# Two-layer transformer: layer 1's second and third block go to the experts as one group, experts at half the rate beside the last two attentions

## Chip, cores and metric

The kernel runs on one core of a Trainium2 chip. The metric is the device time of one execution in microseconds (us); less is better. Engines: PE (matrix multiply, with its weight loads as PEld), DVE (vector), ACT (scalar), POOL (gather and scatter issue, a few small operations), SP (issues the direct transfers).

## What is computed

The input is 8 sequences of 256 tokens with 128 features, 2048 tokens in all. Two layers follow, each an attention and a mixture of experts with 8 experts, of which every token takes two. Cut to what matters here (layer 1; layer 0 has a softmax attention and Gelu experts):

```python
x = x + _L1_attn_ref(_layernorm(x), ...)        # linear attention, 16 heads, segments of 32
x = x + _L1_ffn_ref(_layernorm(x), ...)

def _L1_ffn_ref(x, gate_w, gate_b, w1, b1, w2, b2):
    probs = softmax(xt @ gate_w + gate_b)
    _, idx = top_k(probs, 2)
    mask = one_hot(idx, 8).sum(axis=1) > 0
    h1 = relu(einsum('th,ehf->etf', xt, w1) + b1)     # 128 -> 512 for each expert
    out_e = einsum('etf,efh->eth', h1, w2) + b2       # 512 -> 128
    return einsum('eth,te->th', out_e, mask)
```

## The kernel before

**Blocks and slots.** The 2048 tokens are four blocks of 512 (`NBLK`, four tiles of 128 rows each, `NT`). Layer 1's attention of a block needs that block's layer 0 to be done, and nothing of other blocks. For the experts, the tokens of a block are sorted by expert into slot tiles of 128 rows: `dispatch` (line 380) counts with small matmuls how many tokens chose each expert, gives every expert whole tiles, and works out each token's two rows. 512 tokens with two choices fill at most 2·4 + 8 − 1 = 15 tiles (`SL`), since each expert's last tile may be part empty; the kernel always computes all 15. Eight indirect transfers on POOL (line 433) scatter the rows into a buffer in memory, `xg[h]`; the buffers were filled with zeros at the start.

**A slot tile.** `experts` (line 469) is a generator. Its first step starts the load of four tiles of rows (`xr`, line 477) and the weights of two tiles; its second turns the rows (four transposes on PE, line 487, and a copy on DVE, line 488). Then comes one step for each tile and one more at the end: load the weights of the tile two ahead (`weigh`, two transfers of 256 KB, whose address is read from `half.expert`), four matmuls into the hidden layer (line 508; in f32 each is recorded as two, so 8 a tile), four activations on ACT (line 515), and the second matmuls of the tile before (line 520). After every fourth tile the results are copied out of the accumulator on DVE (line 528) and written to `yg[h]` (line 531). 15 tiles take 18 steps. The row load waits for all scatters of its block.

**Back from the experts.** `chosen` (line 563) gathers each token's two result rows by 8 indirect transfers on POOL (line 569). In layer 0 `combine0` adds them and `before1` prepares layer 1's attention (projections, scores with the segment means, about eight steps); in layer 1 `finish` adds them (line 1349) and stores the block.

**The order of the work.** Each engine runs its instructions in the order in which the program issues them, nearly so at least, and the program chooses that order with two queues (`Lines`, line 1274): "chain" holds routing, gathers, combining and preparing, "experts" the expert generators, one after another. The attentions are generators too: `attention1` (line 1058) has 9 parts (sums, scores of tile 0 to 3 with values and heads one part behind, then `retrieved` for tiles 0 to 3). After each part, `beside` calls `go`:

```python
def go(self, time, chain, experts):
    for _ in range(chain):
        self.now += time / chain
        ...
        self.step("chain")
        self.credit = min(self.credit + experts / chain, 2.0)
        while self.credit >= 1.0:
            self.step("experts")
            self.credit -= 1.0
```

`PART1 = (1.5, 3, 2.0)` stands for layer 1: three chain steps and two expert steps after each part, so 18 expert steps beside one attention, just one block's. A step whose due time has not come is passed over. After the attention of block b, `routed(b, 1)` joins the chain (statistics, logits, the two best experts, `dispatch`), and three time units after its experts are known, its generator may run. The last attention over, `go(*PART1)` runs until both queues are empty; this is called the tail below.

Layer 0's experts run beside layer 0's attention and the first two attentions of layer 1. Layer 1's blocks 0 and 1 go beside attentions 2 and 3, blocks 2 and 3 come in the tail.

Of the kernel before, what the change touches and what calls it, by code (L numbers as in the profile page):

```python
# [54 lines left out]
SL = 2 * NT + E - 1  # L56
# [11 lines left out]
    "before": P, "ones": P, "cap": E * NT, "upto": E * E, "slot": SL, "index": E,  # L68
# [11 lines left out]
def two_layers(  # L80
# [163 lines left out]
    def slots_of_zeros():  # L244

        nc.gpsimd.memset(zero, 0.0)
        for h in range(NBLK):
            xg.append(tl(dram, [SL * P, D], f"xg{h}"))
            rows = xg[h].rearrange("(t p) d -> p t d", p=P)
            filled.append([])  # L250
            for t in range(0, SL, SG):
                n = min(SG, SL - t)
                filled[h].append(
                    nc.sync.dma_start(
                        out=rows[:, t : t + n, :],
                        in_=zero.unsqueeze(1).to_broadcast([P, n, D]),
                    ).ins
                )
            yg.append(tl(dram, [SL * P, D], f"yg{h}"))

# [108 lines left out]

    class Block:  # L370


        def __init__(self, b):
            self.h = b
            self.experts_known = False
            self.rows = tl(wk, [P, NT, D], "hrows")
            self.hots = tl(wk, [P, 2, NT, E], "hhots")
            self.gates = tl(wk, [P, 2, NT], "hgates", bufs=NBLK)

    def dispatch(half, b1s):  # L380

        h1, h2 = half.hots[:, 0], half.hots[:, 1]
        m, tot = small("chosen", (P, NT, E)), small("total", (P, E))
        nc.vector.tensor_tensor(m, h1, h2, ALU.add)
        nc.vector.tensor_reduce(tot, m.rearrange("p t e -> p e t"), AX.X, ALU.add)
        yield
        pr = bank()
        rank = pr[:, 0 : NT * E].rearrange("p (t e) -> p t e", e=E)
        with behind(PE):
            nc.tensor.matmul(rank, lhsT=const("before"), rhs=m, start=True, stop=False)  # L390
            for t in range(NT - 1):
                n = NT - 1 - t
                nc.tensor.matmul(
                    rank[:, t + 1 :, :], lhsT=const("ones"),
                    rhs=m[:, t, :].unsqueeze(1).to_broadcast([P, n, E]),
                    start=False, stop=(t == NT - 2),
                )
            pc = bank()
            nc.tensor.matmul(pc[:, 0:E], lhsT=const("ones"), rhs=tot, start=True, stop=True)

        c3, tiles = small("cap3", (P, E, NT)), small("tiles", (P, E))
        nc.vector.tensor_tensor(
            c3, last(pc[:, 0:E], NT), const("cap").rearrange("p (e c) -> p e c", e=E), ALU.is_gt
        )
        nc.vector.tensor_reduce(tiles, c3, AX.X, ALU.add)
        u3, ends, starts = small("upto3", (P, E, E)), small("ends", (P, E)), small("starts", (P, E))
        nc.vector.tensor_tensor(
            u3, tiles.unsqueeze(1).to_broadcast([P, E, E]),
            const("upto").rearrange("p (e c) -> p e c", e=E), ALU.mult,
        )  # L410
        nc.vector.tensor_reduce(ends, u3, AX.X, ALU.add)
        nc.vector.tensor_tensor(starts, ends, tiles, ALU.subtract)

        base, pos = small("base", (P, E)), small("pos", (P, NT, E))
        nc.vector.tensor_scalar_mul(base, starts, float(P))
        nc.vector.tensor_tensor(
            pos, rank, base.unsqueeze(1).to_broadcast([P, NT, E]), ALU.add
        )
        ph, at = small("posk", (P, 2, NT, E)), small("at", (P, 2, NT))
        nc.vector.tensor_tensor(  # L420
            ph, half.hots, pos.unsqueeze(1).to_broadcast([P, 2, NT, E]), ALU.mult
        )
        nc.vector.tensor_reduce(at, ph, AX.X, ALU.add)
        half.slots = tl(wk, [P, 2, NT], "slots", mybir.dt.uint32, NBLK)
        nc.vector.tensor_copy(half.slots, at)  # L425
        yield

        xg_h = xg[half.h]
        half.sent = []
        key = f"sent{next(names)}"  # L430
        for t in range(NT):
            for k in range(2):
                i = nc.gpsimd.indirect_dma_start(  # L433
                    out=xg_h[:, :],
                    out_offset=bass.IndirectOffsetOnAxis(ap=half.slots[:, k, t : t + 1], axis=0),
                    in_=half.rows[:, t, :], in_offset=None,
                ).ins
                tc.declare_no_dep(i, group=key, reason="slots of their own")
                tc.add_to_no_dep_group(key, i)
                for f in filled[half.h]:  # L440
                    tc.add_manual_dep(i, f.name, SYNC, reason="after zeros")
                half.sent.append(i)
            if t % 2:
                yield

        sl = const("slot").unsqueeze(2).to_broadcast([P, SL, E])
        o1, o2 = tl(wk, [P, SL, E], "own1", bufs=1), tl(wk, [P, SL, E], "own2", bufs=1)
        nc.vector.tensor_tensor(o1, starts.unsqueeze(1).to_broadcast([P, SL, E]), sl, ALU.is_le)
        nc.vector.tensor_tensor(o2, ends.unsqueeze(1).to_broadcast([P, SL, E]), sl, ALU.is_gt)
        nc.vector.tensor_tensor(o1, o1, o2, ALU.mult)  # L450
        nc.vector.tensor_tensor(
            o2, o1, const("index").unsqueeze(1).to_broadcast([P, SL, E]), ALU.mult
        )
        of = small("of", (P, SL))
        nc.vector.tensor_reduce(of, o2, AX.X, ALU.add)
        half.expert = tl(wk, [P, SL], "expert", mybir.dt.int32, NBLK)
        nc.vector.tensor_copy(half.expert, of)
        half.bias = tl(wk, [P, SL, NC], "bias", bufs=NBLK)
        b4 = tl(wk, [P, SL, NC, E], "bias4", bufs=1)
        nc.vector.tensor_tensor(  # L460
            b4, o1.unsqueeze(2).to_broadcast([P, SL, NC, E]),
            b1s.rearrange("p (e c) -> p c e", c=NC).unsqueeze(1).to_broadcast([P, SL, NC, E]),
            ALU.mult,
        )
        nc.vector.tensor_reduce(half.bias, b4, AX.X, ALU.add)
        half.experts_known = True
        yield

    def experts(half, w1, w2, func):

        x_rows = xg[half.h].rearrange("(t p) d -> p t d", p=P)
        y_rows = yg[half.h].rearrange("(t p) d -> p t d", p=P)

        def load(t0):
            n = min(SG, SL - t0)
            xr = tl(wk, [P, SG, D], "xr")
            i = nc.sync.dma_start(out=xr[:, 0:n, :], in_=x_rows[:, t0 : t0 + n, :]).ins
            for s in half.sent:
                tc.add_manual_dep(i, s.name, SYNC, reason="rows sent")
            return xr  # L480

        def turned(xr, t0):
            n = min(SG, SL - t0)
# [7 lines left out]
        def weigh(s):  # L491
            e = nc.values_load(
                half.expert[0:1, s : s + 1], engines=(mybir.EngineType.SP,),
# [9 lines left out]
        def hidden(s, xrT):  # L503
# [9 lines left out]
            for c in range(NC):  # L513
                src, bias = ph[:, c * P : (c + 1) * P], half.bias[:, s, c : c + 1]
                nc.scalar.activation(hT[:, c, :], src, func, bias=bias)  # L515
# [9 lines left out]
        def store(po, t0):  # L525
            n = min(SG, SL - t0)
# [13 lines left out]
        for s in range(SL + 1):  # L540
            if s + AHEAD < SL:
                weigh(s + AHEAD)
            if s < SL:
# [3 lines left out]
                if t0 < SL:  # L547
# [5 lines left out]
            if prev is not None:  # L553
# [4 lines left out]
                if t == SG - 1 or s == SL:  # L558
                    store(po, s - 1 - t)
# [3 lines left out]
    def chosen(half):  # L563

        half.yt = yt = tl(wk, [P, 2, NT, D], "yt")
        for t in range(NT):
            with behind(POOL):
                for k in range(2):
                    nc.gpsimd.indirect_dma_start(  # L569
                        out=yt[:, k, t, :], out_offset=None, in_=yg[half.h][:, :],  # L570
                        in_offset=bass.IndirectOffsetOnAxis(
                            ap=half.slots[:, k, t : t + 1], axis=0
# [306 lines left out]
    def route0(x, half):  # L879
# [17 lines left out]
        half.acc = acc = tl(wk, [P, NT, D], "acc", bufs=NBLK)  # L897
# [4 lines left out]
        yield from dispatch(half, b1s0)  # L902
# [347 lines left out]
    def route1(x, half):  # L1250
# [13 lines left out]
        yield from dispatch(half, b1s1)  # L1264
# [53 lines left out]
    PART0, PART1 = (2.0, 4, 1.5), (1.5, 3, 2.0)  # L1318

    SENT, STORED, BACK = 3, 2, 2  # L1320
    lines, linear = Lines(), {}

    def to_experts(b, half, layer):
        w1, w2, func = ((w1_0, w2_0, AF.Gelu), (w1_1, w2_1, AF.Relu))[layer]
        lines.add("experts", experts(half, w1, w2, func), SENT, lambda: gather(b, half, layer))
# [29 lines left out]
    def routed(b, layer):  # L1355
# [3 lines left out]
        half = Block(b)  # L1359
        sent = (route0, route1)[layer](xs[b], half)  # L1360
        for _ in sent:
            yield
            if half.experts_known:
                to_experts(b, half, layer)
                half.experts_known = False
# [13 lines left out]
    def layer1(b):  # L1379
        while b not in linear:  # L1380
            lines.go(*PART1)
        beside(attention1(linear[b], xs[b]), PART1)
# [10 lines left out]
def shape_constants():  # L1393
# [35 lines left out]
    c["cap"] = np.broadcast_to(P * np.arange(NT), (P, E, NT))  # L1429
# [52 lines left out]
```

## Time and profile before

| | us |
|---|---|
| median of 4 runs | 702.98 (700.52, 700.56, 705.40, 706.04) |
| the profiled execution | 699.48 |
| its span, first to last instruction | 697.7 |

| engine | busy us | share of the span |
|---|---|---|
| PE | 568.4 | 81% |
| PEld (weight loads, beside PE) | 424.6 | 61% |
| DVE | 406.7 | 58% |
| ACT | 333.9 | 48% |
| POOL | 189.9 | 27% |

The mean granted PE clock is 0.923 of full speed. The transfers moved 95.8 MB, 240 x 256 KB of it expert weights. Where things stand in the span: the first scores of layer 1's four attentions (line 1125) start at 322.0, 387.7, 461.5 and 541.4 us; layer 1's scatters start at 439.3, 497.2, 560.3 and 620.7 us, its gathers at 539.3, 601.9, 646.5 and 683.1 us. The last expert matmul ends at 678.5 us.

How to read the lines: a group of instructions has its line, engine, operation, tiles written and read, partitions x elements, count, then busy us and mean ns of one, then the engine's idle time ahead of them and what ended it. Busy times of matmuls overlap in part, since they are pipelined; the busy time of a stretch counts every moment once. The chain of waits follows the work back from the instruction that ended last, at each step to what released it. "issue" is time in which the engine waited for nothing that the profile shows.

### The profile page before, as it was taken

To read this page: it belongs to the slowest core of one execution; us is meant where nothing else is said; L and a number is where in the kernel's file an instruction comes from. 1 tells how busy PE (TensorE), PEld (TensorE's weight loads), DVE (VectorE), ACT (ScalarE), POOL (GpSimd) and SP (SyncE) were. 2 spreads that over 40 slices of the span, in tenths; PEclk is the share of its full clock that TensorE was granted. 3 is DMA by queue.
4 is the path that set the end of the run, shared out by engine and by line. 5 is a ranking of instruction groups with operands and counts; after the bars stand their busy time and mean duration, and the time that the engine had idled before them with its cause. 6 is when DMAs were issued, how large, how long until landed. Compare 5 with 4: busy or idle time off the path is not lost.

```text
span 697.7 us, 13688 instructions
## 1 busy us (share of the span) xinstructions
PE 568.4 (81%) x4846; PEld 424.6 (61%) x4846; DVE 406.7 (58%) x1193; ACT 333.9 (48%) x761; POOL 189.9 (27%) x223
## 2 busy tenths in 40 slices
PE   4777786998989788976899769979988899887880
PEld 3233343667546456645688547757867789886770
DVE  3665666526746556526687378787887776651110
ACT  2142443686958579852555214643345324433340
POOL 4210115002154111441204430415422440431404
PEclk9899989898999899997999979998999979999995
DMA  6700003453254414452435714455565547778861
GB/s 165 209 20 1 1 1 104 143 177 104 62 177 140 129 46 122 122 166 74 132 92 159 223 59 132 147 166 162 156 178 152 176 151 216 234 228 252 263 200 54
DMA packets 132099, 95.81 MB, mean 137 GB/s; under 512 B 8816, under 2 KB 114368, under 8 KB 132032
## 3 DMA queue, kind: packets, MB, share of 16 engines
q1 hardware_dynamic: 127520, 85.58, 41.5%
q0 software_dynamic: 4096, 8.40, 4.1%
q10 hardware_dynamic: 416, 0.96, 0.5%
q8 instruction: 39, 0.64, 0.4%
q14 instruction: 28, 0.23, 0.1%
HBM read 77.87 MB, written 17.04 MB: 136 GB/s over the span
## 4 chain that ended last, share of the span: by engine, by line
PE 46%; DVE 18%; POOL 9%; issue 9%; ACT 9%; DMA 7%; SPq 1%; POOLq 0%; ACTq 0%; DVEq 0%
PE mm L508 10%; PE mm L520 8%; PE sc L790 7%; POOL xg L433 4%; POOL yt L569 3%; DVE at L1130 2%; PE sc L981 2%; DMA yt<-yg,slots 2%; ACT hT L515 2%; ACT at L737 2%; PE sc L1125 2%; DMA w<-in_w 2%; PE mm L1143 2%; POOL rsqrt L277 1%; PE mm L1162 1%
## 5 line engine op out<-in xcount | busy, mean ns | idle before, releaser
L515 ACT ACTIVATE hT<-mm,bias 128x128 f32<-128x128 f32 x480 | 136.3, 371 | 130.3 <-PE mm L508 121.7
L508 PE MATMUL mm<-xrT,w 128*128 128x128 f32 x960 | 137.4, 290 | 18.5 <-DVE xrT L488 12.1
L508 PEld LDWEIGHTS mm<-xrT,w 128*128 128x128 f32 x960 | 123.4, 201 | 33.6 <-DVE xrT L488 16.8
L520 PE MATMUL mm<-w,hT 128*128 128x128 f32 x960 | 136.2, 283 | 5.9 <-ACT hT L515 5.8
L520 PEld LDWEIGHTS mm<-w,hT 128*128 128x128 f32 x960 | 122.4, 196 | 16.1 <-ACT hT L515 14.4
L433 POOL DMA_INDIRECT xg<-hrows,slots x64 | 66.0, 1032 | 109.6 <-DVE slots L425 57.2
L569 POOL DMA_INDIRECT yt<-yg,slots x64 | 61.2, 956 | 102.7 <-DMA yg<-ys 46.1
L737 ACT ACTIVATE at<-sc 128x1024 f32<-128x1024 f32 x48 | 48.8, 1023 | 56.5 <-PE sc L790 56.3
L790 PE MATMUL sc<-qm,kxT 32*128 32x512 f32 x192 | 52.9, 660 | 11.0 <-ACT at L737 4.5
L790 PE MATMUL sc<-km,qT 32*128 32x512 f32 x192 | 54.7, 703 | 3.3 <-DVE qx L698 1.7
L277 POOL TENSOR_TENSOR rsqrt<-rsqrt,mhalf 128x4 f32<-128x4 f32 (+1 forms) x20 | 18.5, 926 | 124.8 <-DVE rsqrt L276 71.3
L698 DVE TENSOR_REDUCE nmax<-sc 128x8 f32<-128x1024 f32 x32 | 38.9, 1221 | 22.7 <-PE sc L790 22.7
L1130 DVE TENSOR_TENSOR at<-sc,consts 128x1024 f32<-128x1024 f32 x32 | 38.1, 1216 | 8.5 <-PE sc L1125 8.2
L515 ACT ACT_TABLE_LOAD x25 | 32.1, 1283 | 13.6 <-PE mm L508 13.2
L528 DVE COPY ys<-mm 128x512 f32<-128x512 f32 (+1 forms) x32 | 20.9, 654 | 30.2 <-PE mm L520 25.0
L790 PEld LDWEIGHTS <-identb 32*32 32x32 bf16 (+1 forms) x320 | 7.8, 92 | 41.0 <-issue 39.5
L1068 POOL TENSOR_TENSOR vm<-va,consts 128x432 f32<-128x432 f32 x16 | 14.6, 932 | 58.2 <-ACT hT L515 19.7
L748 PE MATMUL mm<-at,vx 128*32 128x512 f32 x192 | 26.4, 624 | 4.6 <-ACT at L737 4.6
L790 PEld LDWEIGHTS sc<-qm,kxT 32*128 32x128 f32 x192 | 14.2, 188 | 24.6 <-issue 9.3
L488 DVE COPY xrT<-mm 128x512 f32<-128x512 f32 (+1 forms) x32 | 20.9, 653 | 14.1 <-PE mm L487 14.0
L1149 ACT COPY rope<-mm 128x512 f32<-128x512 f32 x16 | 9.4, 588 | 40.5 <-PE mm L1143 40.5
L1125 PE MATMUL sc<-pqm,kT 32*128 32x512 f32 x128 | 22.1, 764 | 7.3 <-DVE at L1130 4.9
(212 smaller groups left out, 945.1 us busy)
## 6 DMA issues: line engine op xcount, KB each, us to landing
w<-in_w SPq DMA_DIRECT2D x240, 256.0 KB, 3.0
xr<-xg SPq DMA_DIRECT2D x24, 256.0 KB, 4.0
yg<-ys SPq DMA_DIRECT2D x24, 256.0 KB, 2.3
xg<-zero SPq DMA_DIRECT2D x12, 256.0 KB
xr<-xg SPq DMA_DIRECT2D x8, 192.0 KB, 2.4
yg<-ys SPq DMA_DIRECT2D x8, 192.0 KB, 5.0
x<-in_x SPq DMA_DIRECT2D x4, 256.0 KB, 5.5
xg<-hrows,slots POOLq DMA_INDIRECT x64, 2.2
```

What stands on the lines that cost most here:

```text
L277: nc.gpsimd.tensor_tensor(r, r, mhalf[:, 0:n], ALU.pow)
L433: i = nc.gpsimd.indirect_dma_start(out=xg_h[:, :], out_offset=bass.IndirectOffsetOnAxis(ap=half.slots[:, k, t : t + 1], axis=0), in_=half. ...
L508: nc.tensor.matmul(ph[:, c * P : (c + 1) * P], lhsT=w1s[:, c * P : (c + 1) * P], rhs=xrT[:, t * P : (t + 1) * P], start=True, stop=True,)
L515: nc.scalar.activation(hT[:, c, :], src, func, bias=bias)
L520: nc.tensor.matmul(po[:, t * D : (t + 1) * D], lhsT=hT[:, c, :], rhs=w2s[:, c, :], start=(c == 0), stop=(c == NC - 1),)
L569: nc.gpsimd.indirect_dma_start(out=yt[:, k, t, :], out_offset=None, in_=yg[half.h][:, :], in_offset=bass.IndirectOffsetOnAxis(ap=half.slot ...
L698: return nc.vector.tensor_reduce(nm[:, js[0] : js[0] + 2, :], sc.rearrange("p j (i k) -> p j i k", i=G), AX.X, ALU.max, negate=True,)
L737: return nc.scalar.activation(pT[:, js[0] : js[0] + 2, :], sc, AF.Exp)
L748: nc.tensor.matmul(self.po[32 * j : 32 * j + 32, :], lhsT=self.vx[:, kt, j, :], rhs=self.pT_of[s][:, j, :], start=(kt == 0), stop=(kt == qt),)
L790: done[n].append(nc.tensor.matmul(*args, **kw))
L1125: nc.tensor.matmul(sc[j].rearrange("p (i k) -> p i k", i=G), lhsT=pkT[rows, cols], rhs=pqm[rows, :, cols], start=True, stop=True,)
L1130: nc.vector.tensor_tensor(at[:, 2 * a : 2 * a + 2].rearrange("p j i k -> p (j i) k"), d.rearrange("p j (i k) -> p (j i) k", i=G), const("t ...
```

## The change

Layer 1's blocks 1 and 2 are dispatched together. `GROUPS` lists the groups of blocks of each layer; layer 0 keeps one block for each. A `Group` holds the two one-hot choices of all its tiles, and its blocks write their part. `dispatch` runs once for a group, after its last block is routed: with 8 tiles of tokens it has 8 ranking matmuls in place of 4 and one more for the totals, and 16 scatters. 1024 tokens with two choices fill at most 2·8 + 8 − 1 = 23 slot tiles, against 15 + 15. Block 3 is on its own as before. When the group's experts are done, the gathers of both blocks join the chain.

The experts' rate beside the attentions of blocks 2 and 3 falls from two steps a part to one (`PART2`); in the tail it stays two. The buffer `xg1` grows to 23 tiles, so does `yg1`, with two more zero transfers; the constants grow by 40 columns; `acc`, layer 0's accumulator, has three buffers in place of four.

```diff
+GROUPS = (((0,), (1,), (2,), (3,)), ((0,), (1, 2), (3,)))
+MT = NT * max(len(g) for gs in GROUPS for g in gs)
+def slot_tiles(nt):
+    return 2 * nt + E - 1
-SL = 2 * NT + E - 1
+SL = slot_tiles(MT)
...
+    class Group:
+        def __init__(self, h, blocks):
+            self.h, self.blocks, self.parts = h, blocks, []
+            self.nt = NT * len(blocks)
+            self.sl = slot_tiles(self.nt)
+            self.experts_known = False
+            self.hots = tl(wk, [P, 2, MT, E], "hhots")[:, :, 0 : self.nt]
...
-    def dispatch(half, b1s):
+    def dispatch(group, b1s):
+        nt, sl = group.nt, group.sl
...
-            for t in range(NT - 1):
-                n = NT - 1 - t
+            for t in range(nt - 1):
+                n = nt - 1 - t
...
-        for t in range(NT):
+        for t in range(nt):
             for k in range(2):
                 i = nc.gpsimd.indirect_dma_start(
...
-                    in_=half.rows[:, t, :], in_offset=None,
+                    in_=group.parts[t // NT].rows[:, t % NT, :], in_offset=None,
...
-        for s in range(SL + 1):
-            if s + AHEAD < SL:
+        for s in range(sl + 1):
+            if s + AHEAD < sl:
                 weigh(s + AHEAD)
...
-        half.acc = acc = tl(wk, [P, NT, D], "acc", bufs=NBLK)
+        half.acc = acc = tl(wk, [P, NT, D], "acc", bufs=3)
...
-        yield from dispatch(half, b1s1)
+        if half.last:
+            yield from dispatch(half.group, b1s1)
...
-    PART0, PART1 = (2.0, 4, 1.5), (1.5, 3, 2.0)
+    PART0, PART1, PART2 = (2.0, 4, 1.5), (1.5, 3, 2.0), (1.5, 3, 1.0)
...
+        def then():
+            for b, half in zip(group.blocks, group.parts):
+                gather(b, half, layer)
+        lines.add("experts", experts(group, w1, w2, func), SENT, then)
...
-        beside(attention1(linear[b], xs[b]), PART1)
+        beside(attention1(linear[b], xs[b]), PART1 if b < 2 else PART2)
```

## The prediction

> **What bounds the kernel now.** I read the busy time by stretch first, then the chain of waits inside the stretches that the change touches, then their costliest groups, then TensorE's timeline where the stretches meet. Everything up to the end of the second layer-1 attention is issued in the same order by both kernels, so the question starts at 463 us. From 463 to 596 us the last two layer-1 attentions run (blocks 2 and 3), with expert tiles between their steps; from 596 to 680 us there are only expert tiles and the routing of block 3; then come the last gather and store. Columns: stretch, length, busy time of PE, PEld, DVE, ACT and POOL, then granted clock, DMA share, GB/s.
>
> ```profile
> 450.00:500.00 50.00, 42.83 (x443) 35.28 (x442) 42.01 (x122) 20.19 (x55) 14.84 (x16) 0.93 0.51 152
> 463.00:500.00 37.00, 31.19 (x348) 25.97 (x346) 29.65 (x94) 10.99 (x35) 14.84 (x16) 0.91 0.43 127
> 536.00:596.00 60.00, 57.33 (x589) 49.98 (x588) 41.29 (x110) 22.46 (x72) 17.89 (x18) 0.91 0.62 182
> 463.00:596.00 133.00, 119.36 (x1201) 101.84 (x1199) 99.32 (x284) 49.77 (x154) 44.87 (x44) 0.94 0.56 165
> 596.00:640.00 44.00, 36.06 (x295) 34.85 (x295) 19.87 (x64) 17.80 (x62) 17.07 (x17) 0.96 0.78 234
> 640.00:680.00 40.00, 32.00 (x249) 30.07 (x247) 6.18 (x11) 17.11 (x60) 7.61 (x8) 0.96 0.79 239
> ```
>
> In the attentions PE is busy 119.4 of 133 us and DVE 99.3 (0.747 of it; the first row is the most that DVE reaches in any 50 us, 0.84). So PE is the fuller engine, with DVE close behind. In the tail DVE has little to do. Line 508 has 8 matmuls per slot tile; of that line alone the same stretches hold
>
> ```profile
> 463.00:596.00 133.00, 34.17 (x240) 30.83 (x240) 0.94 0.56 165
> 596.00:680.00 84.00, 34.67 (x240) 31.23 (x240) 0.96 0.78 236
> ```
>
> so 30 tiles lie beside the two attentions and 30 in the tail. The chain of waits tells the two attentions apart. The first answer is for 463 to 541 us (attention of block 2), the second for 541 to 597 us (block 3):
>
> ```profile
> by line: PE mm L508 11.6%; issue 7.5%; DVE at L1130 7.3%; PE mm L520 6.6%; POOL xg L433 5.2%; PE sc L981 4.4%; POOL rsqrt L277 4.0%; DVE cand L348 3.2%; DVE vm L1206 3.2%; PE sc L1125 2.7%; DVE hrows L296 2.5%; DVE acc L924 2.2%; DVE hr L12
> ```
>
> ```profile
> by line: PE mm L508 22.9%; PE mm L520 22.9%; issue 10.2%; PE sc L1125 9.3%; PE mm L1143 8.3%; PE mm L1162 8.0%; PE sc L1198 3.4%; PE mm L487 3.2%; ACT hT L515 3.0%; PE mm L587 1.9%; PE mm L602 1.8%; PE mm L1157 1.6%; PE mm L362 1.4%; PE mm
> ```
>
> In the first, expert matmuls are 18% of the chain and DVE's steps carry it; in the second they are 46%. Last, the groups of 463 to 596 us that price a tile:
>
> ```profile
> L520 PE MATMUL mm<-w,hT 128*128 128x128 f32 x247 | 34.9, 281 | 1.9 <-ACT hT L515 1.9
> L508 PE MATMUL mm<-xrT,w 128*128 128x128 f32 x240 | 34.2, 289 | 3.5 <-DVE on L1171 1.5 <-issue 1.3 <-DVE xrT L488 0.8
> L487 PE MATMUL mm<-ident,xr 128*128 128x128 f32 x34 | 5.9, 298 | 0.0
> L528 DVE COPY ys<-mm 128x512 f32<-128x512 f32 (+1 forms) x8 | 5.2, 652 | 1.0 <-PE mm L520 1.0
> L488 DVE COPY xrT<-mm 128x512 f32<-128x512 f32 (+1 forms) x8 | 5.2, 652 | 0.2 <-PE mm L487 0.2
> ```
>
> A tile there costs PE (34.9 + 34.2 + 5.9)/30 = 2.5 us and DVE 10.4/30 = 0.35 us.
>
> **Where the tiles go.** I walked the two queues by the rules in `go` and `step`. Before, the experts of layer-1 blocks 0 and 1 (15 + 15 tiles) fall beside attentions 2 and 3, as the trace has it. After, blocks 1 and 2 are sent only when block 2 is routed, which happens beside attention 3; until then only block 0's 15 tiles exist, and at one step per part nine of them fall beside attention 2 and six beside attention 3. The other 23 + 15 = 38 tiles come in the tail. So the attentions lose 15 tiles and the tail gains 8: the 7 saved tiles are worth something only if the attentions shrink by more than the tail grows.
>
> **The tail: dearer.** Block 3's tiles alone run from 639.4 us (first line-508 matmul) to 678.5 us: 39.1/15 = 2.61 us a tile, PE, weight transfers and row loads together. Eight more: +20.9 us. Bounds: 2.0 us where nothing waits (seven tiles from 598.8 to 612.7 us), +16; 84/30 = 2.8 with routing among them, +22.4. I take 2.61 because most of the new tiles run with no routing beside them. The gather of block 0 (8 indirect DMAs, about 1.25 us each on POOL) and its additions (line 1349, 1.6 us of DVE) also move there, under tiles that last 60 us: nothing, or at most +2 from shared DMA engines; without that cover, 11 us.
>
> **Attention 2: cheaper.** Taking 6 of 15 tiles out of the chain of 463 to 541 us (lines 508 and 520: 9.0 + 5.1 us in it) gives 5.6. The dispatch of block 1 goes from here: its four scatters in the chain with the gaps between them (4.1 + 0.9), which POOL ran ahead of a `rsqrt` that layer 0's last combine waited for, and 2.4 us of its small DVE steps. Together 13.
>
> **Attention 3: cheaper, but DVE is next.** Nine of 15 tiles out of the second chain (12.8 + 12.8 + 1.8 + 1.7 us of lines 508, 520, 487 and 515) would give 17.5. But from 536 to 596 us DVE is busy 41.3 us; nine tiles take 3.1 from it, block 0's additions 1.6, and the wider dispatch (23/15 on lines 448 to 465) adds 1.9: 38.5. At the 0.80 that DVE reaches from 463 to 500 us this needs 48 us of the 60: 12 given back. I take 11.
>
> Both checked together by DVE over 133 us: 99.3 - 15 x 0.35 - 5.6 (one dispatch: half of the paired rows of lines 384 to 465) + 1.9 - 1.6 = 88.8 us of work. At 0.747 that lasts 118.9 us (14 back), at 0.80 it lasts 111 (22 back), at 0.84 105.7 (27 back). PE's own rest, 119.4 - 37.5 + 0.9 (four more dispatch matmuls) = 83 us, is below. My 24 back is a DVE share of 0.815, between the 0.80 of the stretch itself and its best 50 us.
>
> The Trainium skill speaks against this move (Perfetto Trace Analysis, Optimization Strategy): where the fullest engine changes from stretch to stretch, interleaving those stretches can help. The rows above show just that, DVE at 0.75 beside the attentions and near 0.15 from 640 us on, and the change un-mixes eight tiles; by the rule alone the sign would be slower.
>
> **Where they meet.** Before, the tail's first tile waits for its turned rows: PE stood 2.7 us until 598.8 us, under few steps. After, the order is the last `retrieved`, block 3's statistics, then the first turn, with no other tile in flight: the DVE steps ahead (line 1206 twice, lines 1212 and 1215, four statistics) are some 4.5 us. +2.5, between 0 and +5. SP's first row load and both weight loads behind it wait for 16 scatters, at 1.27 us start to start 20 us and 2.2 to land; they start where block 2's did, 19 us after the first scores (541.4 to 560.3), or a little sooner, and so land about 41 us after them, while attention 3 should last 46: hidden by some 5 us.
>
> **The granted clock** was 0.50 from 557 to 567 us, after a PE wait of only 1.9 us (553.2 to 555.0), and that cost some 5 us of PE work. Fewer tiles mean more such waits, on a stretch where DVE would bind: I take 0, up to +5. The skill (TensorE: Matmul & The Clock Gate, The HAM clock gate) has the clock halved after an idle window of about 3.4 us; here a shorter gap came before it, and by the rule fewer windows would be lost than I allow.
>
> Nothing else costs: two more zero transfers of 256 KB for the longer `xg1` and 40 more constant columns land before 100 us, where the DMA share from 50 to 100 us is 0.00. `acc` with 3 buffers makes block 3 wait for block 0's combine, over since about 230 us when block 3 is routed at 348.
>
> **Sum** against the profiled execution (699.48 us, span 697.7): -13 - 11 + 20.9 + 2.5 + 0.5 = 0. The median of the runs is 3.5 above it, 702.98; I forecast 703. By the bounds, the attentions give back 14 to 37 and the tail with its start costs 16 to 30.
>
> **The rivals.** *Faster:* PE alone sets the attentions. For it: PE is busy 90%, and the chain of attention 3 is nearly all PE. Against: DVE would have to work 88.8 us in 95.5, 0.93, which it does nowhere. 37.5 back against 23.4: -14, 689 us. It decides from 30 us given back. *Slower:* the attentions run at the pace of their own DVE steps, each waiting for the one before through PE, ACT or POOL, so that DVE's share stays at 0.747 and only 14 us come back, while 23.4 are added: +9.5, 712 us; at 0.76, above it. Place: 463 to 596 us. For it: DVE's 33 us are the largest part of attention 2's chain, with 8.5 of POOL and 5.7 of issue. Against: a third of PE's work leaves the same stretch. *Late rows:* the 16 scatters end after attention 3 and the tail starts dry; 6 us more than my sum if routing comes late by 11: 709 us. It also caps the first rival. That the tiles are not fewer can be ruled out: 15 + 23 + 15 is written out in `slot_tiles`.
>
> **How the numbers follow.** Forecast 0.41 (697 to 708), faster 0.25, slower 0.25, late rows 0.09 (some half of it over 1%). One per cent, 7 us, is about what a measurement of this kernel can tell from no change. So faster 0.25, within 0.46, slower 0.29. Leaving out a tenth on either side, the range runs from 691 us, inside the faster case, to 714 us, inside the slower one.
>
> **What would show it.** Line 508 has 904 matmuls, some 304 of them in the tail. From the first line-1125 matmul of attention 2 (461.5 us) to the tail's first line-508 matmul there are 137 us now; 115 would be right, under 105 the first rival, over 122 the second. DVE's share there should rise to about 0.8 and the chain of attention 3 should turn from PE to DVE. From the first tile of the tail to the end there are 99 us now; 120 would be right, and a tail at 2.0 us a tile would make me wrong by 5. A first row load that waits for scatters well past attention 3 would show the third.

## The result and the profile after

The changed kernel takes 705.15 us (median of 52 runs), the kernel before 702.92 (78 runs): a ratio of 1.0021 with a 95% interval of 1.0004 to 1.0038. Run again beside other kernels it stood at 1.0079 (1.0048 to 1.0110). So there is no gain, and a loss of some 0.2 to 0.8%. The two intervals do not overlap, so a ratio can shift between sessions by more than its interval says, here by 0.6%. The lines below are from a profiled execution with a span of 706.9 us; line numbers are those of the changed kernel, 24 or 25 higher around the experts (508 is 533, 520 is 545, 487 is 512, 569 is 594).

The stretches, cut where the last two attentions begin (first scores of attention 2) and where the tail's first expert tile starts. Columns: stretch, length, busy time of PE, PEld, DVE, ACT and POOL, granted clock, DMA share, GB/s; then the same for line 533 alone (PE and PEld only).

```profile
468.20:579.80 111.60, 92.77 (x953) 73.72 (x953) 92.26 (x263) 34.06 (x96) 36.05 (x36) 0.91 0.35 103
579.80:706.90 127.10, 86.24 (x676) 83.37 (x676) 28.89 (x79) 43.90 (x154) 39.14 (x41) 0.85 0.70 212
```

```profile
468.20:579.80 111.60, 17.39 (x120) 15.52 (x120) 0.91 0.35 103
579.80:706.90 127.10, 44.80 (x304) 40.85 (x304) 0.85 0.70 212
```

Cut in the same way, the kernel before has 137.3 us (461.5 to 598.8) and 98.9 us (to 697.7). The attentions hold 15 tiles instead of 30 and are 25.7 us shorter; the tail holds 38 instead of 30 and is 28.2 us longer. (In the first profiled execution of the changed kernel, with a span of 709.9 us, the attentions take 116.9 us and the tail 128.0; attention 2 alone took 73.1 us there at a granted clock of 0.81, and 66.9 here at 0.90.) DVE's share beside the attentions is 92.26/111.6 = 0.83. The chain of waits of the two attentions, 468 to 535 us and 535 to 580 us:

```profile
by line: issue 11.8%; PE mm L533 8.2%; DVE at L1156 7.0%; PE sc L1151 6.2%; PE mm L545 5.2%; PE sc L1007 5.1%; DVE vm L1232 5.1%; DVE hr L1238 3.2%; DVE hhots L363 2.5%; POOL norms L986 2.5%; PE mm L1169 2.2%; DVE probs L1031 1.7%; DVE xl L
```

```profile
by line: DMA yg<-ys 10.3%; DVE vm L1232 9.3%; PE mm L533 8.7%; PE mm L1169 6.0%; DVE hr L1238 5.7%; DVE at L1156 5.3%; PE mm L545 5.0%; PE sc L1151 4.9%; issue 4.5%; PE mm L1188 4.4%; PE mm L417 3.4%; ACT hT L540 2.5%; DVE cand L361 2.3%; P
```

In the second, expert matmuls fell from 46% to 14% and DVE's steps lead, but the first entry is new: a store of expert results, `yg<-ys`. It leads to where the tail's extra time is. TensorE's timeline where the tail begins (start, duration, operation, count; in brackets the idle time before it and what ended that):

```profile
577.12 1.09 PE L512 MATMUL mm<-ident,xr 128*128 128x128 f32 x4 [1.56 <-DMA xr<-xg]
579.81 3.78 PE L533 MATMUL mm<-xrT,w 128*128 128x128 f32 x16 [1.60 <-DVE xrT L513]
583.39 1.32 PE L545 MATMUL mm<-w,hT 128*128 128x128 f32 x8
595.47 1.16 PE L324 MATMUL mm<-ident,hrows 128*128 128x128 f32 x4 [10.76 <-DVE hrows L308]
```

After two tiles TensorE stands for 10.76 us: its next instruction in order is the transpose of block 3's normalized rows (line 324, line 312 before), and the other 36 tiles stand behind it. (In the first profiled execution the same wait is 11.12 us.) `hrows` needs POOL's `rsqrt`. POOL's timeline (line 457 is a scatter, 594 a gather, 289 the `rsqrt`), then the issues of SP's queue:

```profile
551.63 2.09 POOL L457 DMA_INDIRECT xg<-hrows,slots  x1 [8.04 <-DVE slots L449]
...
571.70 0.96 POOL L457 DMA_INDIRECT xg<-hrows,slots  x1 [0.30 <-issue]
584.12 0.98 POOL L594 DMA_INDIRECT yt<-yg,slots  x1 [11.47 <-DMA yg<-ys]
...
592.92 0.94 POOL L594 DMA_INDIRECT yt<-yg,slots  x1 [0.30 <-issue]
593.88 1.06 POOL L289 TENSOR_TENSOR rsqrt<-rsqrt,mhalf 128x4 f32<-128x4 f32 x1
```

```profile
558.49 0.34 SPq L522 DMA_DIRECT2D w<-in_w  x1
574.09 0.92 SPq L502 DMA_DIRECT2D xr<-xg  x2
...
578.70 0.46 SPq L556 DMA_DIRECT2D yg<-ys  x1
```

Read from SP on: the group's first row load (line 502) waits for the sixteen scatters, and SP issues nothing from 558.5 to 574.1 us. Block 0's last result store (line 556) stands behind it and goes out at 578.70. The store's data were ready at 572.2 us, when their copy on DVE (line 553) ended; the row load and five weight transfers then went ahead of it, and from its issue to the first gather 5.4 us passed, with a DMA share of 0.96 from 578 to 584 us. Block 0's gathers, next on POOL, wait 11.47 us for that store. Block 3's `rsqrt`, whose operands were ready at 579.2 us, stands behind the eight gathers and runs at 593.88; the last of its operands on VectorE was

```profile
579.00 0.17 DVE L288 TENSOR_SCALAR rsqrt<-mv 128x4 f32<-128x4 f32 x1
```

In the kernel before, that `rsqrt` ran ahead of the gather:

```profile
599.44 1.04 POOL L277 TENSOR_TENSOR rsqrt<-rsqrt,mhalf 128x4 f32<-128x4 f32 x1 [28.57 <-DMA w<-in_w]
601.94 1.02 POOL L569 DMA_INDIRECT yt<-yg,slots  x1 [1.46 <-ACT hT L515]
```

The kernel before has a like knot elsewhere, where layer 1 begins. There the PE, the SP and the POOL timelines read:

```profile
407.90 1.12 PE L312 MATMUL mm<-ident,hrows 128*128 128x128 f32 x4 [9.51 <-DVE xrT L488]
```

```profile
378.00 1.74 SPq L477 DMA_DIRECT2D xr<-xg  x2
380.47 0.44 SPq L531 DMA_DIRECT2D yg<-ys  x1
385.59 0.46 SPq L531 DMA_DIRECT2D yg<-ys  x1
```

```profile
375.63 0.95 POOL L433 DMA_INDIRECT xg<-hrows,slots  x1 [0.30 <-issue]
391.30 0.98 POOL L569 DMA_INDIRECT yt<-yg,slots  x1 [14.71 <-DMA xr<-xg]
...
402.79 1.04 POOL L277 TENSOR_TENSOR rsqrt<-rsqrt,mhalf 128x4 f32<-128x4 f32 x1
```

Scatters, a row load ahead of stores, gathers, `rsqrt`, and a PE wait of 9.51 us on `hrows`. (The label names VectorE's last earlier step; the `rsqrt` at 402.79 shows what was late. The gather's wait is labelled with the row load; that it too waited for the store of 385.59 is read from the order.)

### The profile page after: what moved, and what is told of

Same layout as the page of the kernel before. It is cut to its first block, busy times and chain, and to the rows that moved or that the text cites. A ratio compares the mean times of both kernels' runs of the same rounds, so it can differ in the third digit from the quotient of the medians.

```text
span 709.9 us, 13319 instructions
## 1 busy us (share of the span) xinstructions
PE 567.1 (80%) x4725; PEld 419.4 (59%) x4725; DVE 400.1 (56%) x1169; ACT 326.6 (46%) x733; POOL 188.5 (27%) x223
## 5 line engine op out<-in xcount | busy, mean ns | idle before, releaser
L540 ACT ACTIVATE hT<-mm,bias 128x128 f32<-128x128 f32 x452 | 129.1, 373 | 130.2 <-PE mm L533 125.8
L533 PE MATMUL mm<-xrT,w 128*128 128x128 f32 x904 | 132.1, 293 | 18.5 <-DVE xrT L513 14.0
L533 PEld LDWEIGHTS mm<-xrT,w 128*128 128x128 f32 x904 | 118.7, 205 | 31.3 <-DVE xrT L513 16.6
L545 PE MATMUL mm<-w,hT 128*128 128x128 f32 x904 | 130.3, 287 | 2.3 <-ACT hT L540 2.0
L545 PEld LDWEIGHTS mm<-w,hT 128*128 128x128 f32 x904 | 117.8, 200 | 11.6 <-ACT hT L540 9.9
L815 PE MATMUL sc<-qm,kxT 32*128 32x512 f32 x192 | 55.0, 683 | 11.1 <-ACT at L762 4.6
L815 PE MATMUL sc<-km,qT 32*128 32x512 f32 x192 | 56.8, 726 | 3.2 <-DVE qx L723 1.7
L513 DVE COPY xrT<-mm 128x512 f32<-128x512 f32 (+1 forms) x30 | 19.6, 655 | 18.2 <-PE mm L512 18.1
L308 DVE TENSOR_SCALAR hrows<-x,mv,rsqrt 128x128 f32<-128x128 f32 x32 | 9.2, 344 | 36.4 <-POOL rsqrt L289 36.4
```

Source lines behind the costliest of these rows:

```text
L533: nc.tensor.matmul(ph[:, c * P : (c + 1) * P], lhsT=w1s[:, c * P : (c + 1) * P], rhs=xrT[:, t * P : (t + 1) * P], start=True, stop=True,)
L545: nc.tensor.matmul(po[:, t * D : (t + 1) * D], lhsT=hT[:, c, :], rhs=w2s[:, c, :], start=(c == 0), stop=(c == NC - 1),)
L815: done[n].append(nc.tensor.matmul(*args, **kw))
```

## The experiments

Theory A: the stall at the start of the tail is a queue of orders, and taking it away gives its time back. Rival B: the tail is bound tile by tile, and a wait taken away returns elsewhere. All ratios are to the kernel before in the same session, with 95% intervals. The profiled executions of the group at the full rate and of the later gather are about 1% longer than the medians of their kernels, that of both orders at the full rate 0.6%; their lines are read for order and waits more than for length. Where a stretch is given, "attentions" runs from the first scores of attention 2 to the tail's first tile, "tail" from there to the end of the span.

**The changed kernel again**, unedited, as the measure for the others.

> The changed kernel as it is, for a second profile. Theory A (a new wait eats the gain): PE stands for 10 us or more once at the start of the tail, between the first two tiles of the group and the turning of block 3's rows, because block 0's eight gathers are ahead of block 3's rsqrt on POOL; about 115 us from the first scores of attention 2 to the first tile of the tail, and 0 to +3 us on the kernel before in the median. Rival B (the predicted balance: attentions give back some 20 us, the tail costs about as much tile by tile): that wait belongs to one execution, here it is under 4 us, and the tail is long because a tile costs 2.6 us and more all along.

708.37 us, 1.0079 (1.0048 to 1.0110); the profile shown above. The wait is there again, as theory A has it; the time is 5.5 us above the kernel before instead of 0 to 3.

**Both orders at once.** The gather of block 0 two time units later, so that the `rsqrt` stands ahead of it on POOL; and every group's first row load placed in SP's order where the code issues it, behind the last store of the group ahead (`behind(SP)` keeps it from being moved forward).

```
-        lines.add("chain", chosen(half), STORED, use)
+        lines.add("chain", chosen(half), STORED + 2 * (layer == 1 and b == 0), use)
...
-            i = nc.sync.dma_start(out=xr[:, 0:n, :], in_=x_rows[:, t0 : t0 + n, :]).ins
+            with behind(SP) if t0 == 0 else nullcontext():
+                i = nc.sync.dma_start(out=xr[:, 0:n, :], in_=x_rows[:, t0 : t0 + n, :]).ins
```

> Two orders altered and no work taken away: block 0's gather is due two time units later, so that block 3's rsqrt is ahead of it on POOL; and the group's first row load stands behind block 0's last store on SP. Theory A: the 11 us wait at the start of the tail is gone, and the time falls by 9 to 13 us against the changed kernel, to 0.98 to 0.985 of the kernel before (690 to 694 us). Rival B: the wait moves on to the next row load or weight load, the time stays within 4 us of the changed kernel.

680.9 us, 0.9694 (0.9641 to 0.9747): the sign of theory A with over twice its size. The stall is gone, but attention 2's first scores also came at 448.0 us instead of 468.2, ahead of the place. The next runs take the edit apart.

**The group at the full rate, and half the rate without the group.** The change has two parts; each alone:

```
-        beside(attention1(linear[b], xs[b]), PART1 if b < 2 else PART2)
+        beside(attention1(linear[b], xs[b]), PART1)
```

> The group of 23 tiles without the half rate: two expert steps beside the last two attentions too. Block 0's 15 tiles then all lie beside attention 2, none beside attention 3, and block 0's gather comes beside attention 3, far ahead of the tail. Theory A: no 11 us wait at the start of the tail, so it is 4 to 10 us faster than the changed kernel, although attention 3 has no tiles to fill it. Rival B: an attention 3 without tiles stands on its own DVE steps and saves too little, so it is slower than the changed kernel by 3 to 10 us.

```
-GROUPS = (((0,), (1,), (2,), (3,)), ((0,), (1, 2), (3,)))
+GROUPS = (((0,), (1,), (2,), (3,)), ((0,), (1,), (2,), (3,)))
```

> The half rate without the group: four blocks of 15 tiles, one expert step a part beside the last two attentions. 15 tiles lie beside them and 45 in the tail. Both theories: the tail grows by 15 tiles of 2.6 us (39 us), the attentions give back 15 to 20 us, as DVE paces them and block 1's dispatch stays where it was; 18 to 26 us slower than the kernel before, 1.025 to 1.037. If tiles in the tail cost 2.0 us, only 8 to 12 us slower.

The group at the full rate: 694.05 us, 0.9857 (0.9801 to 0.9913). It too holds 15 tiles beside the attentions (116.8 us) and 38 after them, but block 0's tiles end sooner: their last store goes out at 537.9 us, ahead of the scatters, there is no 11 us wait (TensorE waits 5.79 us for the group's rows instead), and the tail takes 114.8 us. Half the rate without the group: 720.07 us, 1.0243 (1.0174 to 1.0313), with 15 tiles beside (125.3 us) and 45 in a tail of 132.6; the attentions give back 12.0 us and the tail grows by 33.7, where 15 to 20 and 39 were expected. So the grouping gains; the half rate alone only moves fifteen tiles to the tail, and beside the group it is what puts block 0's last store behind the row load.

**The two orders one by one**, in the changed kernel. First only the later gather:

> The changed kernel with one order different: block 0's eight gathers are taken up two time units later, so that block 3's rsqrt stands ahead of them on POOL. Theory A (the 11 us in which PE waits at the start of the tail for block 3's rows are the queue POOL gather -> rsqrt): that wait is gone or under 2 us, the row load of the group still holds SP for some 15 us, and the time is 9 to 12 us below the changed kernel, 693 to 697. Rival B (the tail is bound by the balance of its tiles, a wait taken away comes back tile by tile): 702 to 706, as the changed kernel. Between: the waiting row load holds the last result store and the first weights, a third of the gain is given back, 698 to 701.

699.72 us, 0.9973 (0.9935 to 1.0011). The transpose of line 324 goes without a wait, but SP is still held until 579.87, and a new wait of 4.32 us for the dispatch of block 3 stands at 605.00:

```profile
589.77 0.66 PE L324 MATMUL mm<-ident,hrows 128*128 128x128 f32 x4
...
605.00 2.07 PE L533 MATMUL mm<-xrT,w 128*128 128x128 f32 x8 [4.32 <-DVE cap L426]
```

Of the 9 to 12 us that A expected it shows 3.4 by the ratio to 1.0021 and 7.4 by that to 1.0079; the case named in between came true.

Then only the row load, and only the group's (`t0 == 0 and group.nt > NT` as the condition in the edit above). On PE, POOL and VectorE the order of instructions is exactly that of the changed kernel, and on SP only this load stands elsewhere:

> The changed kernel with one transfer at another place on SP: the first row load of the group of two blocks stands behind block 0's last result store; PE, POOL and VectorE keep their order. Theory A: the store goes out 10 to 15 us earlier, the gathers run under the group's scatters' landing, the rsqrt is early, the 11 us wait is gone, time 693 to 697. Rival B: 702 to 706. If the 27 us that both edits together brought come from this place alone, it would be 678 to 684; I expect not, since in that kernel the first scores of attention 2 began 14 to 20 us earlier than in the changed kernel, ahead of this place.

693.92 us, 0.9901 (0.9870 to 0.9931), inside what A expected and outside what B did. SP's, POOL's and TensorE's timelines at the same place:

```profile
568.64 0.37 SPq L556 DMA_DIRECT2D yg<-ys  x1
572.11 5.05 SPq L502 DMA_DIRECT2D xr<-xg  x3
```

```profile
569.74 0.96 POOL L457 DMA_INDIRECT xg<-hrows,slots  x1 [0.30 <-issue]
571.48 0.98 POOL L594 DMA_INDIRECT yt<-yg,slots  x1 [0.78 <-issue]
...
581.23 1.06 POOL L289 TENSOR_TENSOR rsqrt<-rsqrt,mhalf 128x4 f32<-128x4 f32 x1
```

```profile
575.69 1.09 PE L512 MATMUL mm<-ident,xr 128*128 128x128 f32 x4 [3.72 <-DMA xr<-xg]
577.56 3.78 PE L533 MATMUL mm<-xrT,w 128*128 128x128 f32 x16 [0.78 <-DVE xrT L513]
581.13 1.57 PE L545 MATMUL mm<-w,hT 128*128 128x128 f32 x8
582.81 1.01 PE L324 MATMUL mm<-ident,hrows 128*128 128x128 f32 x4
```

The store goes out ahead of the load, the gathers follow the last scatter with 0.78 us between them, and the transpose of line 324 goes without a wait, 5.3 us after the tail's first tile instead of 15.7. TensorE waits longer for the group's rows, 3.72 us instead of 1.56. The attentions take 117.5 us and the tail 114.5 instead of 127.1. One load moved on one queue is worth 1 - 0.9901/1.0021 = 1.2%, 8.4 us, and against the other measurement of the changed kernel, 1.0079, 1.8%, 12.4 us: about the stall's 10.8 us. With the load behind them the five weight transfers go out earlier too; how much of the gain is theirs was not tried.

**The same order in every group**, in the changed kernel and in the kernel before:

> As the run before, but in every group of both layers the first row load stands behind the last result store of the group ahead of it. The difference from the run before is what the same order brings in the groups of layer 0 and at the start of layer 1. Theory A with this upstream part: 12 to 16 us lower than the run for the group alone, 680 to 685, with the first scores of attention 2 at 448 to 452 us instead of 461 to 468. If the upstream 14 to 20 us are only one execution differing from another: the same as the run for the group alone.

> The kernel before with the same order on SP in every group, without the change. If the gain upstream belongs to the order and not to the grouping: 12 to 20 us below the kernel before, 683 to 691, and the changed kernel with this order is ahead of it by only the rest. If the order helps only where a group has sixteen scatters: 700 to 705, no change.

684.2 us, 0.9761 (0.9725 to 0.9797), and 693.56 us, 0.9882 (0.9843 to 0.9922). The first is by the ratios 1.4% or 9.8 us below the run for the group alone, where 12 to 16 us were expected; the second is 8.3 us below the kernel before, where 12 to 20 were. So the order brings a gain upstream without the grouping, though less than expected. Attention 2's first scores come at 453.6 us in the changed kernel and at 451.7 instead of 461.5 in the kernel before, whose attentions then take 145.3 us instead of 137.3 and give most of it back, while its tail takes 94.5 instead of 98.9. The wait of 9.51 us at the start of layer 1 became 6.05 us there, and 5.21 us in the changed kernel, whose row is

```profile
399.66 1.12 PE L324 MATMUL mm<-ident,hrows 128*128 128x128 f32 x4 [5.21 <-DVE xrT L513]
```

**Both orders in the kernel before**, to see what the grouping is worth by itself:

> The kernel before, without the change, with both orders: first row loads behind the last store in every group, block 0's gather two time units later. There the rsqrt already stood ahead of the gather, so the later gather should bring nothing over the store order alone (693.6): 691 to 696. The changed kernel with both orders had 680.9; the difference, 10 to 15 us, is then what the grouping is worth once its own queue is out of the way. If the grouping is worth nothing by itself and the two orders made the gain: 679 to 684.

691.31 us, 0.9864 (0.9808 to 0.9921). Against 0.9694 with the grouping: 1 - 0.9694/0.9864 = 1.7%, and by the pair with only the row load moved 1 - 0.9761/0.9882 = 1.2%. The second pair is from one session, the first from two. By the medians the grouping is thus worth 8 to 12 us where its own queue is out of the way; in the profiles the stretches from attention 2 on differ by less, 5 us in the pair with both orders and 7 in the other.

**No tile, and full rate**, both with both orders, to price a tile beside the attentions:

```
-    PART0, PART1, PART2 = (2.0, 4, 1.5), (1.5, 3, 2.0), (1.5, 3, 1.0)
+    PART0, PART1, PART2 = (2.0, 4, 1.5), (1.5, 3, 2.0), (1.5, 3, 0.0)
```

> The changed kernel with both orders and no expert tile beside the last two attentions; all 53 of layer 1 from block 0 on stand in the tail. It shows the attentions' bare length, and so what a tile beside them costs. With half the rate it was 118.3 us from attention 2's first scores to the tail with 15 tiles among them. If the attentions go at their own DVE pace and the tiles lie in PE's gaps: 108 to 118 us here, the tail 30 us longer, 700 to 711. If PE sets the pace (1.6 to 1.9 us of the path a tile): 90 to 95 us, and 680 to 690.

> The changed kernel with both orders and the last two attentions at the full rate of two steps a part instead of one: block 0's 15 tiles all go beside attention 2, and tiles of the group of 23 beside attention 3 as soon as it is known. If a tile costs the same beside an attention as in the tail (about 2 us of the end, the balance of the prediction): 678 to 684, as with half the rate. If DVE sets the attentions' pace and PE has room there: 672 to 677. If PE sets it and a tile beside them costs more than in the tail: 685 to 690.

With no tile: 712.0 us, 1.0122 (1.0033 to 1.0210). With `PART2` equal to `PART1`: 688.43 us, 0.9807 (0.9747 to 0.9867). The stretches of three kernels that all have both orders, in this order: no tile beside the attentions, 15 tiles (the grouping at half the rate), 30 tiles (the kernel before). Columns as above.

```profile
451.50:553.90 102.40, 76.86 (x699) 52.52 (x699) 85.17 (x248) 17.67 (x36) 36.34 (x36) 0.73 0.10 31
553.90:710.20 156.30, 117.76 (x932) 113.52 (x931) 35.57 (x94) 61.45 (x214) 39.64 (x41) 0.87 0.76 229
```

```profile
448.00:566.30 118.30, 98.35 (x954) 78.89 (x954) 94.34 (x263) 34.09 (x96) 37.02 (x37) 0.86 0.37 109
566.30:680.10 113.80, 83.47 (x676) 80.69 (x676) 28.81 (x79) 44.03 (x154) 38.73 (x41) 0.87 0.78 229
```

```profile
451.30:592.80 141.50, 121.47 (x1212) 103.73 (x1211) 102.70 (x294) 51.63 (x156) 44.87 (x44) 0.93 0.57 165
592.80:688.50 95.70, 67.14 (x540) 65.05 (x540) 24.95 (x74) 34.99 (x122) 32.24 (x33) 0.87 0.70 211
```

The bare attentions take 102.4 us with DVE busy 0.83 of it. The first fifteen tiles beside them add 15.9 us, 1.06 each; the next fifteen, with a second dispatch, 23.2 us, 1.55 each. In the tail, eight tiles (30 to 38) add 18.1 us, 2.26 each, and fifteen more (38 to 53) 42.5, 2.83 each, of which 12.1 are two waits for row loads. Half the rate without the group, against the kernel before, gives 12.0/15 = 0.80 us beside the attentions and 33.7/15 = 2.25 in the tail. So the attentions are the cheaper place for a tile. The granted clock beside the attentions is 0.73, 0.86 and 0.93 in the three kernels, and the prices hold its part too. The bare length of 102.4 us lies between the two expectations, 108 to 118 us if DVE sets the pace and 90 to 95 if PE does; the time, 712.0 us, is just above the first. DVE was the fuller engine there (0.83, PE 0.75), which fits the first, but that it sets the pace is not shown by this alone. At the full rate the tiles beside the attentions are again fifteen, since the group is not known earlier, but all of them fall ahead of attention 3 (stretches cut at its first scores):

```profile
456.00:529.00 73.00, 64.60 (x623) 54.03 (x623) 57.01 (x161) 30.41 (x87) 16.98 (x17) 0.91 0.42 124
529.00:578.70 49.70, 37.21 (x334) 26.59 (x334) 38.66 (x109) 4.12 (x9) 28.16 (x28) 0.61 0.25 74
```

Attention 2 takes 73.0 us with fifteen tiles and attention 3 takes 49.7 with none; at half the rate they take 70.9 with ten tiles and 47.3 with five. At the full rate the scatters start 22.4 us after attention 3's first scores (18.7 at half), and TensorE waits 4.59 us for the group's rows. That the tiles of the group would lie beside attention 3, as the expectation had it, did not happen. A second profiled execution was to say whether the long attention 3 belongs to the kernel:

> The kernel with both orders and the full rate once more, unedited, for a second profiled execution: in the first, attention 3 without a tile among its steps took 49.7 us at a granted clock of 0.61, against 41.9 us at 0.70 in the kernel that has no tile beside either attention. If that belongs to the kernel (the scatters start late, and the tail waits for the group's rows): 48 to 51 us again, a wait of 4 to 6 us for the rows, 685 to 691 in all. If it was that one execution: 42 to 46 us, and 681 to 685.

757.59 us, with the kernel before at 753.88 in that session, 51 us above its time elsewhere: 1.0043 (1.0002 to 1.0084). It can't answer. The profile has gaps of a kind that no other one here shows, such as

```profile
604.70 1.22 PE L627 MATMUL mm<-wot,oT 128*128 128x128 f32 x4 [11.40 <-issue]
```

eleven microseconds within attention 3 for which no releaser is seen. Attention 3 takes 58.5 us there, 47.1 without that gap, and its granted clock is 0.63. Why the full rate was slower than the half rate (0.9807 against 0.9694, in two sessions) stays open: late rows and a low clock are seen, but neither was tried alone.

The fastest kernel of the study is thus the changed one with both orders, 680.9 us.

## Why the prediction came out as it did

The total was right (703 forecast, 705.15 measured), and in part by luck, since the sum behind it was not: a stall of 10.76 us was missing from it, and a gain that it put at zero stood against that stall. With both orders, where the stall is gone, the profiles show -23.2 us in the attentions and +18.1 in the tail, 5 us of gain; the sum had -21.5 and +21.4 for them (24 less 2.5, and 20.9 with a further 0.5 for which it names no row). Of the rest of the 8 to 12 us, 3.3 lie ahead of attention 2 in this pair; what remains is not placed.

**Where the tiles go: right.** Line 533 has 120 matmuls beside the attentions and 304 after them, as named; ten tiles lie beside attention 2 and five beside attention 3 (80 and 40 matmuls), where nine and six were named.

**The attentions: right in their sum.** 115 us were named from first scores to the tail; 111.6 and 116.9 were measured in the two executions of the changed kernel, 117.5 with the row load moved. Between the two kernels with both orders the attentions give back 141.5 - 118.3 = 23.2 us, against 24 less the 2.5 of the tail's start; attention 2 gives 9.1 of them where 13 were named, and attention 3 14.0 where 11 less 2.5 were. DVE's share rose to 0.83, and 0.79 with the row load moved, where about 0.8 was forecast, and the chain of attention 3 turned from expert matmuls to DVE's steps. This rules out both main rivals: DVE did not go to 0.93, nor did it stay at 0.747.

**Eight tiles in the tail at 2.61 us: mis-sized.** They cost 2.26 us each between the kernels with both orders, 114.0 - 94.5 = 19.5 us, 2.44 each, between the two with the row load moved in every group, and 114.5 - 98.9 = 15.6 us, 1.95 each, between the kernel before and the changed one with the group's row load moved. That makes the term 1 to 5 us too dear. I read it so: the price came from block 3's stretch, which holds a group's own start and end, and more tiles in a group pay these no second time; this was not tried alone.

**The gather of block 0 "under tiles that last 60 us: nothing": the step that failed.** Only its additions were hidden (line 1381, 1.67 us at 597.27, beside TensorE's work). Its eight gathers fill POOL from 584.1 to 593.9 us, and TensorE stands from 584.7 to 595.5. I asked what the gathers cost and what covers them, and not what stands behind them on POOL: block 3's `rsqrt`, and through it TensorE's next instruction, with all the tiles that were to be the cover behind that. The price for lost cover, 11 us, was named and is the stall's length, 10.76 us; what was missed is that the cover goes. A moved step is to be followed on each in-order queue to the instruction behind it, and the row for this one lay in the trace of before, the 9.51 us at 407.90. The moved row load shows 8 to 12 us of the time hanging on it.

**Late rows: half right.** The last scatter starts 36.7 us after attention 3's first scores (535.05 us), and the row load lands at 577.1, 42 us after them; 41 was forecast. Attention 3 lasts 44.8 us, where 46 was. TensorE lost only 1.56 us to the rows. But that waiting load had SP, with the store behind it, and there the loss arose. The rival saw the wait and looked at the wrong follower.

**The clock.** A row of 3 us each, as the tail begins:

```profile
577.00:580.00 3.00, 1.27 (x5) 0.90 (x6) 2.65 (x8) 0.00 (x0) 0.00 (x0) 0.52 0.91 263
...
598.00:601.00 3.00, 3.00 (x17) 3.00 (x16) 1.50 (x4) 1.14 (x4) 0.00 (x0) 0.50 0.47 134
601.00:604.00 3.00, 3.00 (x28) 3.00 (x29) 1.63 (x9) 1.12 (x5) 0.00 (x0) 1.00 0.58 159
```

After the 10.76 us wait the clock stays at 0.50 for 5.5 us of work (595.47 to 601), which is some 2.8 us of PE's work lost and part of the stall's price. It fits the forecast's 0 to +5. The Trainium skill (TensorE: Matmul & The Clock Gate, The HAM clock gate) gives the full clock after at least one busy window of about 3.4 us. The 5.5 us fit that; the kernel before fits it less well, where the clock stood at 0.50 from 557 to 567 us with TensorE busy all the time.

**The rule on mixing stretches.** The Trainium skill (Perfetto Trace Analysis, Optimization Strategy) says that interleaving stretches with different fullest engines may help. The kernel with no tile beside the attentions agrees: 712.0 us (1.0122) against 680.9 (0.9694). It did not decide the change, since the fifteen tiles and the dispatch that left the attentions weigh more than the eight un-mixed: -23.2 us there, +18.1 in the tail.

So without the knot the change gains about 1.2 to 1.7%; near zero is the sum of that gain and a stall which the half rate made. Not settled is how the 3 us between the two kernels with the row load moved in all groups and with both orders divide: the intervals, 0.9725 to 0.9797 and 0.9641 to 0.9747, overlap.

## What to carry to other kernels

When a step moves, write down for each queue that runs in order what comes right behind it and who waits for that; its own duration may be hidden while its place in the queue is not. A load that must wait for scatters belongs behind the stores that are ready to go, since a waiting issue holds what comes after it on its queue (here SP issued nothing for 15.6 us). Before you price such a thing from a guess, look for the same sequence elsewhere in the trace: here it stood, as a wait of 9.51 us, at 408 us in the trace of before. The same order in every group helped the kernel before as well, by 1.2%, though that wait only fell to 6.05 us.

## What the hardware showed that was not expected

TensorE's clock was already at about half from 577 us, with PE waits of only 1.56 and 1.60 us around it, so here it fell without a long gap. In attention 3 a higher granted clock went with tiles among its steps: 0.79 to 0.98 with five, in six executions; 0.61 to 0.66 with none, in three at the full rate; 0.70 with none in the kernel without tiles, whose attention 3 at 41.9 us was still the shortest. So a low clock alone did not make that stretch long. And a whole session can be 7% slower for both kernels, with TensorE gaps of 10.81 and 11.40 us that the profile puts down to no engine and no transfer; what they are was not tried.
